# One layernorm's transposes derived from another's in an attention and mixture-of-experts block

## The chip, the cores and the metric

The kernel runs on one core of a Trainium2 chip. The metric is the device time of one execution in microseconds (us), from the device's own clock. A core has five engines that work side by side, each through its own list of instructions in order: TensorE (PE: matmuls and transposes), VectorE (DVE), ScalarE (ACT), GpSimd (POOL) and SyncE (SP). DMA transfers are issued by SP, ACT or POOL and carried out by 16 DMA engines. TensorE writes to PSUM, whose banks of 128 x 512 f32 (the kernel uses eight) must be read out ("evicted") by VectorE or ScalarE before they can be used again.

## What is computed

Everything is f32. x has 2 x 2048 tokens of width 256.

```python
xn = layernorm(x)                                  # first layernorm
# attention: 16 heads of 16, Chebyshev features of order 6, prefix sums instead of a softmax
qkv = xn @ W_in.T ; ... ; attn = (num / den) @ W_out.T
# feed-forward on xn
xf = layernorm(xn) * ln_w + ln_b                   # second layernorm
e = argmax(xf @ router_w) ; s = sigmoid(max(xf @ router_w))
routed = silu((s*xf) @ gate[e]) * ((s*xf) @ up[e]) @ down[e]      # one of 8 experts per token
shared = silu(xf @ sh_gate) * (xf @ sh_up) @ sh_down
out = x + attn + xn + routed + shared
```

With m and v the mean and variance of a token's row, r0 = 1/sqrt(v + 1e-5) is the scale of the first layernorm. The second layernorm, applied to the first's result, is z = (x - m) * r1 with a scale r1 of its own that follows from v alone: r1 = 1/sqrt(v(1 + 1e-5) + 1e-10). So xn and z are the same row (x - m) with two scales, and xn = z * (r0 / r1).

## The kernel before

The 4096 tokens are cut into 8 chunks of 512 (`CH`), each of 4 tiles of 128. Layouts: a tile has tokens on the partitions; matmuls want the features there, so each chunk's z and xn are transposed on TensorE into xfT and xnT (two halves k of 128 features by 512 tokens).

*The front* (L453 to L579), in three groups of chunks, [0], [1, 2, 3] and [4, 5, 6, 7]. `stat` (L455) takes mean and variance on VectorE; `roots` (L464) gets r0 and r1 (`rs`) from a square root on ScalarE and a Newton step on VectorE, and `nm` from them (L486, L487). `front(c)` (L491) makes xn on ScalarE (L499, four activations per chunk) and z on VectorE (L507, into `zall`), transposes both on TensorE (L519: for each of the two, two halves of four 128 x 128 transposes, each half into one PSUM bank), and evicts: xfT on ScalarE with ln_w and ln_b (L523), xnT on ScalarE or VectorE (L527, L529). z goes to DRAM for later gathers (L530), xfT and xnT of chunks 1 to 7 too (L569, L571). The router multiplies xfT for each pair of chunks (L542), transposes the result (L550) and adds the logits on VectorE (L558, L559). X, which collects the output, is set on ScalarE (L564).

*Constants* on GpSimd (L287 to L342): identity, ones, then heads, weigh, shift, spread, upper for the attention and the routing, all at the very start.

*Routing* (`route`, L582) ranks tokens by expert and builds tables of 36 tiles of 128 slots: 28 full tiles with one expert each (`NFULL`) and 8 tiles whose two halves have different experts.

*Attention* (`attend`, L825): per chunk, QKV matmuls (L848), Chebyshev features, prefix scans on VectorE (L915) and small matmuls (L878 to L986).

*Experts* (`expert`, L1012): SP loads the weights of a tile in three pieces of 512 KB per expert (L1030, L1036), out of a pool `w_p` of 8 pieces that grows by 10 when the attention is done; GpSimd gathers z rows (L1041) and scatters the result (L1087); TensorE transposes (L1049), multiplies (L1059, L1080) and transposes (L1072). A tile of two experts loads six pieces and its matmuls have 64 output rows, in pairs. *Shared expert* (`shared`, L785): L794 and L811 per chunk, held back for the last two chunks (`hold`). Last, SP reads the scattered rows, VectorE adds them and SP stores the output (L1107 to L1121).

*Order.* All this is entered as operations with a cost, a priority and the data and buffers that they need; `Plan.order` (L157) lays them out greedily in time and so fixes each engine's list of instructions before anything runs. A lower `prio` comes first; `alt` names a second engine that may take an operation. Once fixed, an engine that waits for one instruction waits with all behind it. Six PSUM banks (`bank_p`) are shared by nearly everything; a bank is free when every operation that uses it is done.

Of the kernel before, what the change touches and what calls it, by code (L numbers as in the profile page):

```python
# [11 lines left out]
F32 = mybir.dt.float32  # L12
I32 = mybir.dt.int32
AF = mybir.ActivationFunctionType
ALU = mybir.AluOpType
# [5 lines left out]
P = 128  # L21
NB, S, D = 2, 2048, 256
# [3 lines left out]
CH = 512  # L26
# [229 lines left out]
def kernel(  # L256
# [25 lines left out]
    y_dram = dram.tile([NTOK, D], F32, name="y_dram")  # L282
    xn_dram = [dram.tile([P, KD, CH], F32, name=f"xn_dram_{c}") for c in range(NC)]
# [9 lines left out]

    heads = const.tile([P, 56], F32, name="heads")
    nc.gpsimd.affine_select(
        out=heads, in_=ones[:, :56], pattern=[[-DH, 56]], compare_op=ALU.is_ge,
        fill=0.0, base=24 * DH, channel_multiplier=1,
    )
    nc.gpsimd.affine_select(
        out=heads, in_=heads, pattern=[[DH, 56]], compare_op=ALU.is_ge,  # L300
        fill=0.0, base=DH - 1 - 24 * DH, channel_multiplier=-1,
    )

    sqb = const.tile([P, 2], F32, name="sqb")
    nc.gpsimd.memset(sqb[:, 0:1], sq4[1])
    nc.gpsimd.memset(sqb[:, 1:2], sq5[1])

    HB = NH // KD  # L310
    weigh = const.tile([P, QD], F32, name="weigh")
    nc.gpsimd.memset(weigh, 0.0)
    for lo, n, base, wt in [(0, NH, QD * i, wts[i + 1]) for i in range(4)] + [
            (g * HB, HB, QD * g + NH, wts[5]) for g in range(KD)]:
        nc.gpsimd.affine_select(
            out=weigh[:, lo : lo + n], in_=weigh[:, lo : lo + n], pattern=[[-1, n]],
            compare_op=ALU.not_equal, fill=wt, base=-base, channel_multiplier=1,
        )

    shift = const.tile([P, 1], F32, name="shift")  # L320
    nc.gpsimd.memset(shift, 0.0)
    nc.gpsimd.memset(shift[QD : QD + NH, :], -DH * off[2])
    nc.gpsimd.memset(shift[3 * QD : 3 * QD + NH, :], -DH * off[4])

    spread = const.tile([P, KD * P], F32, name="spread")
    nc.gpsimd.memset(spread, 1.0)
    for i in range(NT):
        rows = spread[ts(i, QD), :]
        nc.gpsimd.affine_select(
            out=rows, in_=rows, pattern=[[1, KD * P]], compare_op=ALU.is_ge,  # L330
            fill=0.0, base=0, channel_multiplier=-DH,
        )
        nc.gpsimd.affine_select(
            out=rows, in_=rows, pattern=[[-1, KD * P]], compare_op=ALU.is_ge,
            fill=0.0, base=DH - 1, channel_multiplier=DH,
        )

    upper = const.tile([P, P], F32, name="upper")
    nc.gpsimd.affine_select(
        out=upper, in_=ones[:, :P], pattern=[[1, P]], compare_op=ALU.is_gt,  # L340
        fill=0.0, base=0, channel_multiplier=-1,
    )  # L342
# [16 lines left out]
    nm = const.tile([P, 2, NTT], F32, name="nm")  # L359
# [19 lines left out]
    def cut(n):  # L379
        nonlocal at  # L380
        at += n
        return wide[:, at - n : at]

    xn_p = Pool([cut(NT * D) for _ in range(2)])
# [25 lines left out]
    plan.begin["POOL"] = 7.5  # L410
# [42 lines left out]
    xfTs, xnTs, spilled, fronts = {}, {}, [], []  # L453

    def stat(c):  # L455
        for t in range(NT):
            i = c * NT + t

            def f(c=c, t=t, i=i):
                V.bn_stats(stats[:, i, :], X[c][:, t, :])  # L460
                V.bn_aggr(mv[:, i, :], stats[:, i, :])
            op("DVE", 0.58, f, r=[("X", c, t)], w=[("mv", i)], prio=FRONT + 0.1 * c)

    def roots(cs):  # L464
        a, b = cs[0] * NT, (cs[-1] + 1) * NT
        n = slice(a, b)
        keys = [("mv", i) for i in range(a, b)]
        p = FRONT + 0.1 * cs[0] + 0.01

        def f():  # L470
            V.tensor_scalar(ve[:, 0, n], mv[:, n, 1], EPS, None, ALU.add)
            V.tensor_scalar(ve[:, 1, n], mv[:, n, 1], 1.0 + EPS, EPS * EPS, ALU.mult, ALU.add)
        op("DVE", 0.35, f, r=keys, w=[("ve", a)], prio=p)
        op("ACT", 0.21, lambda: A.activation(rs[:, :, n], ve[:, :, n], AF.Sqrt),
           r=[("ve", a)], w=[("rs", a)], prio=p, table="sqrt")

        def h():
            r_, u_, v_ = rs[:, :, n], nu[:, :, n], ve[:, :, n]
            V.reciprocal(r_, r_)

            V.tensor_tensor(u_, r_, r_, ALU.mult)
            V.tensor_tensor(u_, u_, v_, ALU.mult)
            V.tensor_scalar(u_, u_, -0.5, 1.5, ALU.mult, ALU.add)
            V.tensor_tensor(r_, r_, u_, ALU.mult)

            V.scalar_tensor_tensor(nm[:, 0, n], mv[:, n, 0], -1.0, rs[:, 0, n], ALU.mult, ALU.mult)  # L486
            V.tensor_scalar(nm[:, 1, n], rs[:, 0, n], 1.0, None, ALU.add)  # L487
        op("DVE", 1.2, h, r=[("ve", a), ("rs", a)] + keys, w=[("nm", a // NT + k) for k in range(len(cs))],
           prio=p)

    def front(c):  # L491
        xn4 = Buf(xn_p, f"xn_{c}")
        v4 = lambda b: b.t.rearrange("p (t d) -> p t d", t=NT)
        p = FRONT + 0.1 * c + 0.02
        for t in range(NT):
            i = c * NT + t

            def f(t=t, i=i):
                A.activation(v4(xn4)[:, t, :], X[c][:, t, :], AF.Identity,  # L499
                             bias=nm[:, 0, i : i + 1], scale=rs[:, 0, i : i + 1])  # L500
            op("ACT", 0.59, f, r=[("X", c, t), ("nm", c)], w=[(xn4, t)], prio=p,
               alloc=[xn4] if t == 0 else [])
        for t in range(NT):
            i = c * NT + t

            def f(t=t, i=i):
                V.tensor_scalar(zall[:, i, :], X[c][:, t, :], mv[:, i, 0:1], rs[:, 1, i : i + 1],  # L507
                                ALU.subtract, ALU.mult)
            op("DVE", 0.4, f, r=[("X", c, t), ("nm", c)], w=[("z", i)], prio=p)
        xnT, xfT = Buf(xnT_p, f"xnT_{c}"), Buf(xfT_p, f"xfT_{c}")  # L510
        v2 = lambda b: b.t.rearrange("p (k t) -> p k t", k=KD)
        for nx in (1, 0):
            for k in range(KD):
                bk = Buf(bank_p, f"tr_{c}_{nx}_{k}")

                def f(bk=bk, k=k, nx=nx):
                    for t in range(NT):
                        src = zall[:, c * NT + t, ts(k, P)] if nx else v4(xn4)[:, t, ts(k, P)]
                        T_.transpose(bk.t[:, ts(t, P)], src, ident)  # L519
                op("PE", 4 * MT, f, r=[("z", c * NT + t) if nx else (xn4, t) for t in range(NT)],  # L520
                   w=[bk], alloc=[bk], prio=p)
                if nx:
                    op("ACT", 0.65, lambda bk=bk, k=k: A.activation(  # L523
                        v2(xfT)[:, k, :], bk.t, AF.Identity, bias=lnb[:, k : k + 1], scale=lnw[:, k : k + 1]),
                       r=[bk, "ln"], w=[(xfT, k)], alloc=[xfT] if k == 0 else [], prio=p)
                else:
                    op("ACT", 0.58, lambda bk=bk, k=k: A.copy(v2(xnT)[:, k, :], bk.t),  # L527
                       r=[bk], w=[(xnT, k)], alloc=[xnT] if k == 0 else [], prio=p,
                       alt=[("DVE", 0.68, lambda bk=bk, k=k: V.tensor_copy(v2(xnT)[:, k, :], bk.t))])  # L529
# [31 lines left out]
        for t in range(NT):  # L561
            i = c * NT + t
            kw = dict(bias=nm[:, 0, i : i + 1], scale=nm[:, 1, i : i + 1])
            op("ACT", 0.59, lambda t=t, kw=kw: A.activation(X[c][:, t, :], X[c][:, t, :], AF.Identity, **kw),  # L564
               r=[("nm", c)], w=[("X", c, t)], prio=ROUTE + 1.0)
# [8 lines left out]
    for cs in ([0], [1, 2, 3], [4, 5, 6, 7]):  # L574
        for c in cs:
            stat(c)
        roots(cs)
        for c in cs:
            front(c)  # L579


    def route():  # L582
# [64 lines left out]
        op("PE", 0.9, f, r=["m"], w=[rank, total], alloc=[rank, total], prio=R)  # L647
# [137 lines left out]
    def shared(c, gate):  # L785
# [19 lines left out]
        for tp in range(NT // 2):  # L805
            po = Buf(bank_p, f"po_{c}_{tp}")

            def mm(po=po, tp=tp):
                for i in range(2):
                    for f in range(KF):  # L810
                        T_.matmul(po.t[:, ts(i, D)], hT[f].t[:, ts(tp * 2 + i, P)], sd[:, f, :],  # L811
                                  start=(f == 0), stop=(f == KF - 1))
            op("PE", 8 * M256, mm, r=hT + ["sd"], w=[po], alloc=[po], prio=SHA + c - 0.2)
            accumulate(c, tp, po)
# [10 lines left out]
    def attend(c, gate):  # L825
# [9 lines left out]
        for g in range(KD):  # L835
# [7 lines left out]
            for i in range(3):  # L843
# [6 lines left out]
                o = op("PE", 2 * MM, mm, r=[(xnT, 0), (xnT, 1), "w_in"], w=[pm],  # L850
# [161 lines left out]
    def expert(j):  # L1012
        e = 0.1 * j
# [79 lines left out]
    for j in range(NJ):  # L1093
        expert(j)
# [3 lines left out]
    gate, hold = [], {NC - 2: ups[-6], NC - 1: ups[-3]}  # L1098
# [4 lines left out]
    for c in range(NC):  # L1103
# [15 lines left out]
        n = 2 if c == NC - 1 else NT  # L1119
        for t in range(0, NT, n):  # L1120
# [43 lines left out]
```

## Time and profile before

| what | value |
|---|---|
| runs | 587.37, 589.61 and 2120.74 us; median 589.61 |
| profiled execution | 588.28 us, span from first to last instruction 586.6 us |
| granted TensorE clock | 0.999 |
| TensorE's first instruction / last matmul group begins | 8.97 / 575.38 us |
| instructions | 7613 |

Times in the profile are microseconds from the start of the span unless they are marked ns. In lists of engines, each entry is busy time, share of the span and number of instructions. In the view by slices the span is cut into 40 equal parts, and a digit is the busy share in tenths. In the view of waits a line is "who waited <- for whom: us in total, times, longest". In a timeline a line begins with start and duration; `x8` are eight instructions in a row, and an f32 matmul is recorded as two. `out<-in` are buffers; `L519` is the line of the kernel. PEld is the load of a matmul's stationary operand, beside PE. SPq and ACTq are DMA issues.

### The profile page before, as it was taken

The numbers are of one execution on the slowest core, as the hardware profiler recorded it, in microseconds if no ns is written. First come the engines' busy times: TensorE is split into PE (matmuls) and PEld (weight loads), VectorE is DVE, ScalarE is ACT, GpSimd is POOL, SyncE is SP. The second block draws the span as 40 slices with busy tenths as digits, with TensorE's granted clock in tenths as the row PEclk, the third lists the DMA queues.
The fourth block names the chain that finished last, engine by engine and source line by source line (L and its number), as shares of the span: only waits on it lengthen the run. The fifth ranks groups of instructions, "written<-read, shape, count | busy, mean of one in ns | idle before, by whom it ended". The sixth has DMA issues, their size and how long they took to land.

```text
span 586.6 us, 7613 instructions
## 1 busy us (share of the span) xinstructions
PE 570.6 (97%) x2492; PEld 318.8 (54%) x2492; DVE 486.7 (83%) x785; ACT 252.2 (43%) x494; POOL 96.1 (16%) x106
## 2 busy tenths in 40 slices
PE   3999999999999999999999999999999999999997
PEld 2467566746455545656554554564646544644565
DVE  6889889899999989999999999998999898222254
ACT  5799981135533732542364272355236222112100
POOL 4000000302112033003112302311230313010100
PEclk9999999999999999999999999999999999999999
DMA  8788704517374274418525455572652677995096
GB/s 271 237 307 302 284 1 144 195 56 226 98 234 159 93 230 161 148 53 284 186 102 196 161 165 161 189 241 92 196 176 76 186 256 217 359 377 191 0 356 217
DMA packets 73048, 111.15 MB, mean 189 GB/s; under 512 B 5293, under 2 KB 44463, under 8 KB 73008
## 3 DMA queue, kind: packets, MB, share of 16 engines
q1 hardware_dynamic: 68704, 101.72, 52.2%
q0 software_dynamic: 3456, 8.92, 4.6%
q8 instruction: 20, 0.33, 0.2%
q14 instruction: 20, 0.16, 0.1%
q10 hardware_dynamic: 848, 0.01, 0.1%
HBM read 90.71 MB, written 20.45 MB: 190 GB/s over the span
## 4 chain that ended last, share of the span: by engine, by line
PE 62%; DMA 1%; issue 1%; DVE 0%; POOL 0%; POOLq 0%; DVEq 0%
PE bank L1059 16%; PE bank L794 10%; PE bank L1080 9%; PE bank L848 9%; PE bank L811 6%; PE bank L986 4%; PE bank L1072 2%; PE psk L878 2%; PE psq L878 1%; PE bank L1049 1%; DMA wide<-z_dram,take_i 1%; PE psk L891 1%; PE psk L972 1%; PE bank L959 0%; DMA y_dram<-wide,give_i 0%
## 5 line engine op out<-in xcount | busy, mean ns | idle before, releaser
L1059 PE MATMUL bank<-big,wide 128*128 128x512 f32 (+1 forms) x308 | 121.9, 595 | 0.0
L1087 POOL DMA_INDIRECT y_dram<-wide,give_i x34 | 44.1, 1296 | 333.2 <-ACT carry L921 121.7
L848 PE MATMUL bank<-xnT,w_in 128*128 128x512 f32 x192 | 86.5, 594 | 0.0
L915 DVE TENSOR_TENSOR_SCAN tv<-ones,carry,tv 128x512 f32<-128x512 f32 x60 | 76.6, 1277 | 1.1
L1059 PEld LDWEIGHTS bank<-big,wide 128*128 128x128 f32 (+1 forms) x308 | 47.1, 175 | 55.2 <-issue 52.7
L1080 PE MATMUL bank<-big,wide 128*128 128x256 f32 (+1 forms) x312 | 65.1, 385 | 0.0
L794 PE MATMUL bank<-xfT,sg 128*128 128x512 f32 x128 | 60.8, 597 | 0.0
L794 PE MATMUL bank<-xfT,su 128*128 128x512 f32 x128 | 60.7, 596 | 0.0
L1041 POOL DMA_INDIRECT wide<-z_dram,take_i x34 | 41.0, 1206 | 112.6 <-DVE wide L772 102.5
L1080 PEld LDWEIGHTS bank<-big,wide 128*128 128x128 f32 (+1 forms) x312 | 47.5, 175 | 20.7 <-issue 11.5
L811 PE MATMUL bank<-sd,hT 128*128 128x256 f32 x256 | 57.9, 381 | 0.0
L848 PEld LDWEIGHTS bank<-xnT,w_in 128*128 128x128 f32 x192 | 35.7, 190 | 38.2 <-issue 36.1
L811 PEld LDWEIGHTS bank<-sd,hT 128*128 128x128 f32 x256 | 47.8, 190 | 10.7 <-issue 4.5
L1065 ACT ACTIVATE wide<-bank,slot_s 128x512 f32<-128x512 f32 x35 | 24.1, 688 | 65.9 <-PE bank L1059 65.9
L800 ACT ACTIVATE hT<-bank 128x512 f32<-128x512 f32 x32 | 19.1, 597 | 65.2 <-PE bank L794 63.3
L935 DVE TENSOR_TENSOR o<-o,tv 128x512 f32<-128x512 f32 x64 | 44.2, 690 | 1.9
L1067 DVE SCALAR_TENSOR_TENSOR wide<-bank,slot_s,wide 128x512 f32<-128x512 f32 x35 | 25.9, 739 | 17.9 <-PE bank L1059 17.6
L819 DVE TENSOR_TENSOR X<-X,bank 128x512 f32<-128x512 f32 x32 | 21.8, 680 | 22.1 <-PE bank L811 18.4
L870 DVE SCALAR_TENSOR_TENSOR T<-T 128x1024 f32<-128x1024 f32 x32 | 38.1, 1215 | 0.2 <-ACT T L863 0.2
L794 PEld LDWEIGHTS bank<-xfT,sg 128*128 128x128 f32 x128 | 23.0, 190 | 25.3 <-issue 24.5
L794 PEld LDWEIGHTS bank<-xfT,su 128*128 128x128 f32 x128 | 23.1, 190 | 24.3 <-issue 23.5
L1052 ACT ACTIVATE wide<-bank,lnb,lnw 128x128 f32<-128x128 f32 x72 | 29.1, 458 | 10.3 <-PE bank L1049 10.3
(197 smaller groups left out, 813.8 us busy)
## 6 DMA issues: line engine op xcount, KB each, us to landing
big<-in_up_w SPq DMA_DIRECT2D x39, 512.0 KB
big<-in_down_w SPq DMA_DIRECT2D x39, 512.0 KB
big<-in_gate_w SPq DMA_DIRECT2D x38, 512.0 KB
z_dram<-big SPq DMA_DIRECT2D x8, 512.0 KB
X<-in_x SPq DMA_DIRECT2D x7, 512.0 KB
xf_dram<-xfT SPq DMA_DIRECT2D x7, 512.0 KB
xn_dram<-xnT SPq DMA_DIRECT2D x7, 512.0 KB
xfT<-xf_dram SPq DMA_DIRECT2D x7, 512.0 KB
```

Of the source, the lines that this page charges most:

```text
L794: T_.matmul(b.t, wt[:, k, ts(f, P)], vx(k), start=(k == 0), stop=(k == KD - 1))
L811: T_.matmul(po.t[:, ts(i, D)], hT[f].t[:, ts(tp * 2 + i, P)], sd[:, f, :], start=(f == 0), stop=(f == KF - 1))
L848: T_.matmul(pm.t, w_in[:, k, ds(i * D + g * P, P)], xnT.t[:, ts(k, CH)], start=(k == 0), stop=(k == KD - 1))
L870: op("DVE", 1.27, lambda i=i, j=j, q=part: V.scalar_tensor_tensor(q[i](), q[j](), off[i], q[1](), ALU.subtract, ALU.mult), r=[(T, j)] + X2 ...
L915: o_ = op("DVE", 1.25, lambda b=b, i=i, g=g: V.tensor_tensor_scan(b.t, ones[:, 0:1].to_broadcast([P, CH]), b.t, 0.0 if opening else old[:, ...
L935: op("DVE", 0.66, lambda o=o, b=b: V.tensor_tensor(o(), o(), b.t, ALU.add), r=[b, ok], w=[ok], prio=p)
L1041: op("POOL", 1.28, lambda: G.indirect_dma_start(out=zt.t, out_offset=None, in_=z_dram, in_offset=bass.IndirectOffsetOnAxis(ap=take_i[:, j ...
L1052: op("ACT", 0.46, lambda k=k: A.activation(xT.t[:, ts(k, P)], pz.t[:, ts(k, P)], AF.Identity, bias=lnb[:, k : k + 1], scale=lnw[:, k : k + ...
L1059: T_.matmul(b.t[n, :], xT.t[:, ds(k * P + n.start, n.stop - n.start)], wt.t[:, ts(k, FF)], start=(k == 0), stop=(k == KD - 1), skip_group_ ...
L1067: op("DVE", 0.75, lambda: V.scalar_tensor_tensor(sl.t, pu.t, sc(), sl.t, ALU.mult, ALU.mult), r=[pu, zt, sl], w=[sl], prio=EXQ)
L1080: T_.matmul(py.t[n, :D], hmT.t[:, ds(i * P + n.start, n.stop - n.start)], wd.t[:, ts(i, D)], start=(i == 0), stop=(i == KF - 1), skip_grou ...
L1087: y_ins.append(G.indirect_dma_start(out=y_dram, out_offset=bass.IndirectOffsetOnAxis(ap=give_i[:, j : j + 1], axis=0), in_=yt.t, in_offset ...
```

## The change

Four things are changed.

1. xn is no longer made and transposed. `roots` also computes ratio = r0/r1 (from r1 times its argument times r0), ScalarE writes it to DRAM token by token (`ratio_dram`), and reads it back for each chunk as a row of 512 broadcast to 128 partitions (`rows`). xnT is then VectorE's product of the transposed z in PSUM and that row (new L497). z may be made on ScalarE too for chunks 1 to 7, and the xfT eviction may go to VectorE. In chunk 0 the second half of xfT is on VectorE.
2. The constants after `rw` are made later on GpSimd, once `nm` of chunk 0 is there; statistics get an earlier priority; `roots` is cut in two.
3. The eight tiles of two experts no longer come last but are spread among the full ones, and the held chunks of the shared expert wait for other tiles.
4. The last pair of the shared expert's down products is cut into two, each with its own add, and the last two tiles are stored one by one.

In the changed kernel L487 are the transposes, L490 and L492 the xfT evictions, L497 the xnT evictions, L456 and L463 the ratio's write and read, L470 and L474 z, L511 the router's matmuls, L814 and L831 the shared expert, L876 QKV, L906 the head sums, L1077, L1087, L1100 and L1108 the experts' TensorE work.

```diff
+    ratio_dram = dram.tile([NTOK], F32, name="ratio_dram")
...
-    xn_p = Pool([cut(NT * D) for _ in range(2)])
+    ratio_p = Pool([cut(CH) for _ in range(4)])
...
-    plan.begin["POOL"] = 7.5
+    plan.begin["POOL"] = 2.0
...
-            op("DVE", 0.58, f, r=[("X", c, t)], w=[("mv", i)], prio=FRONT + 0.1 * c)
+            op("DVE", 0.58, f, r=[("X", c, t)], w=[("mv", i)], prio=FRONT + 0.1 * c - 0.3)
...
+            V.scalar_tensor_tensor(nm[:, 2, n], mv[:, n, 0], -1.0, rs[:, 1, n], ALU.mult, ALU.mult)
+            V.tensor_tensor(ratio[:, n], rs[:, 1, n], ve[:, 1, n], ALU.mult)
+            V.tensor_tensor(ratio[:, n], ratio[:, n], rs[:, 0, n], ALU.mult)
...
+        op("ACT", 0.45, lambda: A.dma_start(
+            out=ratio_dram[a * P : b * P].rearrange("(t p) -> p t", p=P), in_=ratio[:, n]),
+           r=[("ratio", a)], w=[("ratio_dram", c) for c in cs], nbytes=64 * KiB, prio=p)
...
-                A.activation(v4(xn4)[:, t, :], X[c][:, t, :], AF.Identity,
-                             bias=nm[:, 0, i : i + 1], scale=rs[:, 0, i : i + 1])
...
+        rows = Buf(ratio_p, f"ratio_{c}")
+        op("ACT", 0.4, lambda: A.dma_start(
+            out=rows.t, in_=ratio_dram[c * CH : (c + 1) * CH].unsqueeze(0).to_broadcast([P, CH])),
+           r=[("ratio_dram", c)], w=[rows], alloc=[rows], nbytes=256 * KiB, prio=p)
...
+            if c:
+                op("ACT", 0.59, f_, r=[("X", c, t), ("r", c), ("nm", c)], w=[("z", i)], prio=p, alt=[("DVE", 0.36, f)])
+            else:
+                op("DVE", 0.36, f, r=[("X", c, t), ("r", c)], w=[("z", i)], prio=p)
...
+        for k in range(KD):
+            bk = Buf(bank_p, f"tr_{c}_{k}")
+            def f(bk=bk, k=k):
+                for t in range(NT):
+                    T_.transpose(bk.t[:, ts(t, P)], zall[:, c * NT + t, ts(k, P)], ident)
...
+            op(*on[k if c == 0 else 0], r=[bk, "ln"], w=[(xfT, k)],
+               prio=p if c else -2.0, alt=on[1:] if c else [])
+            op("DVE", 0.69, lambda bk=bk, k=k: V.tensor_tensor(v2(xnT)[:, k, :], bk.t, rows.t, ALU.mult),
+               r=[bk, rows], w=[(xnT, k)], prio=p)
...
+    def constants():
+        ins = nc.gpsimd.affine_select(
+            out=heads, in_=ones[:, :56], pattern=[[-DH, 56]], compare_op=ALU.is_ge,
+            fill=0.0, base=24 * DH, channel_multiplier=1,
+        ).ins
+        tc.add_manual_dep(ins, begun[0].name, mybir.DependencyInfo(
+            mybir.DependencyClass.Sync, mybir.DependencyReason.DATA))
...
+    op("POOL", 6.5, constants, r=[("nm", 0)], w=["constants"], prio=FRONT)
...
+            if (c, tp) == (NC - 1, NT // 2 - 1):
+                for i in range(2):
+                    op("PE", 4 * M256, lambda i=i, mm=mm: mm([i]), r=hT + ["sd"], w=[(po, i)],
+                       alloc=[] if i else [po], prio=SHA + c - 0.2)
+                    op("DVE", 0.42, lambda i=i, po=po, xs=X[c][:, 2 * tp + i, :]: V.tensor_tensor(
+                        xs, xs, po.t[:, ts(i, D)], ALU.add), r=[(po, i)], a=[("X", c, 2 * tp + i)], prio=SHQ)
+                continue
...
-    for j in range(NJ):
-        expert(j)
-    gate, hold = [], {NC - 2: ups[-6], NC - 1: ups[-3]}
+    n2 = NJ - NFULL
+    tiles = sorted(range(NJ), key=lambda j: j if j < NFULL else (j - NFULL + 0.5) * NFULL / n2 - 0.25)
+    for n, j in enumerate(tiles):
+        expert(n, j)
+    gate, hold = [], {NC - 2: ups[-9], NC - 1: ups[-2]}
...
-        n = 2 if c == NC - 1 else NT
-        for t in range(0, NT, n):
+        for t, n in ((0, 2), (2, 1), (3, 1)) if c == NC - 1 else ((0, NT),):
```

## Prediction, made before the changed kernel was run

> **What bounds the kernel now.** I read four views: busy time per engine, the 40 slices, TensorE's waits, and TensorE's timeline for starts.
>
> ```profile
> PE 570.6 (97%) x2492; PEld 318.8 (54%) x2492; DVE 486.7 (83%) x785; ACT 252.2 (43%) x494; POOL 96.1 (16%) x106
> ...
> PE   3999999999999999999999999999999999999997
> ...
> DVE  6889889899999989999999999998999898222254
> ```
>
> TensorE works without a break from the first slice to the last. A busy PE can hide short stalls, because the ends of matmuls are modelled, so I also took distances between starts: a 128x512 record starts every 0.43 us nearly everywhere, which is its own time. The waits say the same:
>
> ```profile
> PE bank L519 <- POOL wide L614: 9.0, 1, 9.0
> PE bank L1049 <- DMA wide<-z_dram,take_i: 2.2, 2, 1.4
> PE bank L1072 <- DVE wide L1067: 0.6, 1, 0.6
> ```
>
> After its first instruction at 8.97 us TensorE stands for 2.8 us in all. So the span is a head (until the first real matmul), the sum of TensorE's instructions, its few stalls, and a tail after its last matmul. VectorE (DVE) is full to nine tenths from 40 to 490 us but idles at the end: it matters only where TensorE's fixed order meets a late result.
>
> **The change, part by part**, against the profiled execution: 588.28 us, span 586.6, so 1.7 lie around it. It sits between the two ordinary runs (587.37 and 589.61; the median, 589.61, is the upper one because of an odd run of 2120).
>
> *1. Transposes.* 64 of the 128 front transposes (L519, those that read xn) go; counted in both kernels' instructions, nothing else on TensorE changes in number.
>
> ```profile
> 8.97 2.20 PE L519 MATMUL bank<-ident,big 128*128 128x128 f32 x8 [8.97 <-POOL wide L614]
> 10.96 1.75 PE L519 MATMUL bank<-ident,wide 128*128 128x128 f32 x8
> 12.54 1.88 PE L794 MATMUL bank<-xfT,sg 128*128 128x512 f32 x4
> 14.26 10.46 PE L848 MATMUL bank<-xnT,w_in 128*128 128x512 f32 x24
> ...
> 51.08 1.04 PE L519 MATMUL bank<-ident,wide 128*128 128x128 f32 x8
> 51.95 1.04 PE L519 MATMUL bank<-ident,big 128*128 128x128 f32 x8
> ```
>
> The first number is the start. Eight take 51.95 - 51.08 = 0.87 us, 0.11 each. Of the 64, 56 lie in the gapless part: 56 x 0.11 = **-6.2**. The other eight (10.96 to 12.54) belong to the head.
>
> *2. Head.* The root chain is slowed by GpSimd's constants: the same multiply takes 0.379 us in the head and 0.183 later.
>
> ```profile
> L481 DVE TENSOR_TENSOR nu<-rs x3: 183/191/379, 6.8 to 44.3; 128x8 f32<-128x8 f32 x1, 128x24 f32<-128x24 f32 x1, 128x32 f32<-128x32 f32 x1
> ```
>
> The late constants free it. rs leaves ScalarE at 6.54 as before (the sqrt table, 4.84 to 6.12, sets that); reciprocal and four steps at the later spacing (0.24, then 0.21 each) let z start at 7.67, not 8.41. Transposes start at about 8.2 and end at 10.4. But then VectorE's order puts two statistics pairs of chunk 1 ahead of its half of xfT, and chunk 1 lands at about 10.55 (L460 waited for it until 10.57; the third pair starts at 11.66). So that half ends at 11.66 + 0.69 = 12.35 and its matmul starts at 12.5, as before; only the matmul of the other half (two records, 0.86) gets done in the gap: -0.9. Against this: row 10.96 shows transposes at 0.20 each, row 12.54 matmuls at full speed, 3.6 us after TensorE's first work. [...] The new head has holes of about 0.8 and 0.4 us in it. [...] The holes are short: I take 0.6. Head: **-0.3** (-0.9 to +0.8).
>
> *3. Half tiles between the others.* A half tile's matmuls use 64 columns in pairs, and going in and out of that form costs time:
>
> ```profile
> 526.24 3.58 PE bank L1059 x16
> 529.83 1.91 PE bank L794 x4
> ...
> 545.56 1.72 PE bank L1059 x4
> ```
>
> 16 half records take 3.58 instead of 16 x 0.215 = 3.44, and the L794 group after them 1.91 instead of 1.72: about 0.34 per stretch. In TensorE's order there are 12 such stretches before and 16 after: 4 x 0.34 = **+1.4**. The stall of 0.8 at 519 us (a gather behind six weight pieces per half tile) should go: **-0.8**. Against that, a half tile takes 6 of the 8 weight pieces that exist during attention, so stalls of that kind can come earlier: -2.5 (the two at 192 and 216 us go) to +4 (half a microsecond on each of eight); I take 0.
>
> *4. The ratio's way through DRAM.* ScalarE loses 32 xn activations (0.59 each) and 4 evictions, gains 8 of z, and issues 11 DMAs at 0.45 us (L426): 5 us, hidden, as it is 43% busy. VectorE evicts all 16 xnT halves (12 before) and 5 of xfT, loses 8 of z at 0.33, and has 9 small steps more: about +5 us in a stage where it isn't full. But two waits are new: ScalarE's read of the rows stands in its queue until the write has landed, and VectorE's xnT eviction stands until the read has. The write is of 4-byte elements: 512, 1536 and 2048 of them, that is 32, 96 and 128 per DMA engine. Rows for the cost:
>
> ```profile
> q1 hardware_dynamic: 68704, 101.72, 52.2%
> ...
> q10 hardware_dynamic: 848, 0.01, 0.1%
> ```
>
> ScalarE's queue (q10) has mostly 4-byte reads: 0.1% x 16 x 586.6 / 848 = 11 ns a packet; SP's (q1) 71 ns. ScalarE's router load was issued at 4.35, 2.2 us after the end of an earlier small one: I take 2.2 us as latency. So the third write lands 2.2 + 128 x 11 ns = 3.6 us after issue. [...] SP's queue is busy then (DMA slices 8 of 10). If each 4-byte packet waits for one of SP's: 128 x 82 ns + 2.2 = 12.7 us; for the groups of 1536 and 512, 10.1 and 4.8 instead of 3.3 and 2.6.
>
> Group 0: issued at about 10.3, rows needed at 25.5 by the first L876; ScalarE must be free for silu by 18.5. Covered either way. Group 1 to 3: ScalarE issues at about 31.7 (after the v eviction of the tenth QKV matmul). TensorE next needs ScalarE behind its read for the bank of row 45, at about 42.2: landed at 35.0 nothing, at 41.8 plus three issues and three activations 2.7 us. Group 4 to 7: here the banks run out. In the new order TensorE's transposes of chunks 4, 5 and 6 fill all six banks, and each bank is kept until xfT and xnT are out of it; the next TensorE instruction (the router's, L511) needs the first of them. I laid VectorE's order end to end with the rows' durations: ratio ready at 47.0; then 13 z (0.33), hT, one xfT, logits, one 1.22 step, and the first xnT ends at 57.7. TensorE comes to the logits' bank at 54.4 (free at 55.7) and to L511 at 56.1 (free at 57.9): 1.3 + 1.8 = 3.1 us idle where before there was none. That is without any late transfer: the write is issued at 49.8, lands at 53.4, the read at 57.0. Landed at 62.4 instead, L511 waits until 67: 11 us. I take 3.1 plus 0.9 for some of the alternation, **+4.0** (0 to +14), nearer to the q10 row because that is the same queue and the same size of element.
>
> *5. Tail.*
>
> ```profile
> 582.49 0.69 DVE L819 TENSOR_TENSOR X<-X,bank 128x512 f32<-128x512 f32 x1 [1.63 <-PE bank L811]
> 583.21 0.37 SPq L1121 DMA_DIRECT2D out<-X  x1
> ```
>
> The last add shrinks from 0.69 to 0.42 and the last store from 256 to 128 KB (at the 359 GB/s of the busy slices 0.36 us less, partly taken by one more issue of 0.37): **-0.5**. Constants on GpSimd: the same work, 2 to 8 us becomes 9 to 16; the first reader is L511 or L906 beyond 40 us, and GpSimd's next job is a gather at 110 us: 0.
>
> Sum: -6.2 - 0.3 + 1.4 - 0.8 + 4.0 - 0.5 = -2.4; 588.3 - 2.4 = 585.9, say **586**.
>
> **Rivals.**
> *A, likeliest:* most of the 7 us of transposes comes back as a bank stall in the front. 586, own range 582 to 590.
> *B, no stall:* VectorE is quicker than I laid it and the rows come in time; 588.3 - 6.4 = 582, with stalls in the experts gone too 579. For it: before, the same stage has no TensorE wait at all. Against it: six banks, six transposes.
> *C, slower:* the 2048 small writes alternate with SP's packets; +14 instead of +4, 596. It has one place, L511 behind the third ratio write. From 3.6 us of landing on, each further microsecond adds one to the end; at about 6 us more the gain is gone. [...]
> *D, slower:* half tiles starve of weights. Three MB per half tile at the 280 GB/s of early slices are 11 us, while 8 pieces let little be fetched ahead; 2 us a tile are +16: 602. Against it: attention leaves 50 us per chunk and its DMA share is only half.
>
> **How the numbers follow.** A 0.55, B 0.20, C 0.17, D 0.08. The time is A's, 586. The range takes in B down to 579 and C up to 597. A measurement of this kernel tells about 2% from no change: under 577.8 or over 601.4 against 589.6. Faster than that needs B with every stall gone and no cold clock: 0.05. Slower: most of D, the end of C: 0.08. Within: 0.87.
>
> **What would show it.** Right: TensorE's busy time about 7 us lower; two or three TensorE waits on VectorE between 50 and 60 us at L511 and L487; first long matmuls at 11 to 12.5 us. ScalarE's wait at L463 tells how long the small writes take: under 4 us speaks for A or B, 8 to 13 for C. Waits of TensorE on weights at L1087 or L1108 speak for D. The prediction is wrong if TensorE's idle time after 9 us is under 2 us, or if the new idle time lies elsewhere than at these lines.

## The result and the profile after

The changed kernel takes **616.43 us** (616.32 to 617.95 in four runs) against 589.48 before (four runs, one more than in the table above): ratio 1.0476, 95% interval 1.0442 to 1.0509. It is 27 us slower; the forecast was 586.0 with a range of 579 to 597. Here and below a ratio is formed from the fast runs alone, without odd or slow ones, and so differs a little from the quotient of the medians. The profiled execution took 616.51 us, its span 614.8 against 586.6.

The page of the changed kernel: busy time per engine, then TensorE, the granted clock and the bytes moved by slices (15.4 us each here), and ScalarE's DMA queue.

```profile
PE 575.5 (94%) x2428; PEld 315.7 (51%) x2428; DVE 490.3 (80%) x795; ACT 232.9 (38%) x460; POOL 94.3 (15%) x106
...
PE   4596849999999999999899989999999999999997
...
PEclk9797959999999999999999999999999999999999
...
GB/s 272 184 56 201 131 371 154 138 92 80 206 136 162 264 188 78 223 299 19 170 264 182 111 211 190 123 247 174 71 255 169 134 188 259 269 351 173 18 274 281
...
q10 hardware_dynamic: 6144, 2.12, 1.5%
```

64 matmul records fewer, and yet TensorE is busy 4.9 us longer. The large holes are all in the first six slices, up to about 92 us, and in the same slices the clock falls: TensorE stands, and when it gets work again it runs at half speed for a while (the granted clock is 0.50 from 24 to 30, 54 to 64 and 78 to 91 us). From the seventh slice on the row looks like that of before. TensorE's waits:

```profile
PE bank L487 <- DVE big L470: 8.2, 1, 8.2
PE bank L814 <- ACT hT L820: 6.4, 1, 6.4
PE bank L487 <- ACT big L474: 6.2, 1, 6.2
PE bank L487 <- ACT T L887: 4.1, 1, 4.1
PE bank L1077 <- DMA wide<-z_dram,take_i: 3.5, 3, 1.6
PE bank L511 <- DVE xnT L497: 3.4, 1, 3.4
PE bank L487 <- DVE xnT L497: 1.8, 1, 1.8
```

The first is the start (9.0 before). The rest, with three smaller ones of 0.5 to 0.9, are 27.5 us where before there were 2.8. That closes the account: 24.7 more waiting, 4.9 more busy time, 0.7 earlier start, 0.5 shorter tail (from the last matmul group's start to the end 10.76 against 11.22) make +28.4; the span grew by 28.2.

Two chains lie behind this. One is the wait that was forecast: ScalarE's read of the rows stands behind the write. ScalarE's timeline (ACTq lines are DMA issues):

```profile
9.64 0.38 ACTq L456 DMA_DIRECT2D ratio_dram<-ratio  x1
...
24.91 0.34 ACTq L463 DMA_DIRECT2D wide<-ratio_dram  x1
25.29 1.28 ACT L820 ACT_TABLE_LOAD   x1 [12.41 <-DMA ratio_dram<-ratio]
26.58 1.08 ACT L820 ACTIVATE hT<-bank 128x512 f32<-128x512 f32 x2
...
41.02 0.37 ACTq L456 DMA_DIRECT2D ratio_dram<-ratio  x1
...
52.66 1.64 ACTq L463 DMA_DIRECT2D wide<-ratio_dram  x3
...
66.57 0.38 ACTq L456 DMA_DIRECT2D ratio_dram<-ratio  x1
...
78.46 0.38 ACTq L463 DMA_DIRECT2D wide<-ratio_dram  x1
```

From the issue of the write to the issue of its read 15.3, 11.6 and 11.9 us pass, for 512, 1536 and 2048 elements. Four times the elements don't take longer: this is no price per packet. Behind the first read stands silu (L820), and behind silu TensorE's 6.4 us at L814. The 4.1 and 6.2 us at L487 stand behind ScalarE's second and third read in the same way, and the 1.8 us for xnT behind the rows, for which VectorE waits 8.8 us.

The other chain does not pass through the ratio's reader. VectorE's statistics wait for x itself:

```profile
13.53 0.18 DVE L420 BATCH_NORM_AGGREGATE mv<-stats 128x2 f32<-128x6 f32 x1
23.26 0.43 DVE L419 BATCH_NORM_STATS2 stats<-X 128x6 f32<-128x256 f32 x1 [9.54 <-DMA X<-in_x]
```

In the kernel before, the same record (chunk 2) starts 7.7 us earlier:

```profile
15.56 0.43 DVE L460 BATCH_NORM_STATS2 stats<-X 128x6 f32<-128x256 f32 x1 [1.57 <-DMA X<-in_x]
```

SP issues these loads, on another queue. What became of them shows in the stretches of 2 us, of which the last three columns are the granted clock, the DMA engines' busy share (it can pass 1) and GB/s. Before:

```profile
16.00:18.00 2.00, 2.00 (x6) 0.93 (x5) 1.66 (x7) 0.70 (x2) 0.00 (x0) 1.00 1.10 348
```

After:

```profile
14.00:16.00 2.00, 2.00 (x3) 0.71 (x3) 0.00 (x0) 0.00 (x0) 1.70 (x6) 1.00 1.64 261
16.00:18.00 2.00, 2.00 (x5) 0.86 (x4) 0.00 (x0) 0.00 (x0) 0.19 (x1) 1.00 1.19 30
18.00:20.00 2.00, 2.00 (x6) 0.95 (x5) 0.00 (x0) 0.00 (x0) 0.00 (x0) 1.00 1.14 49
20.00:22.00 2.00, 0.81 (x2) 0.00 (x0) 0.00 (x0) 0.00 (x0) 0.00 (x0) 1.00 1.29 74
22.00:24.00 2.00, 0.00 (x0) 0.00 (x0) 0.61 (x2) 0.00 (x0) 0.00 (x0) 0.82 0.99 81
...
45.00:50.00 5.00, 5.00 (x24) 3.73 (x22) 4.17 (x13) 0.00 (x0) 0.00 (x0) 1.00 0.64 7
```

The DMA engines count as fully busy and move 30 to 81 GB/s instead of 348, for 8 us, after a write of 2 KB. After the second write it is 7 GB/s, at a busy share of 0.64. I call this the slump.

### The profile page after: what moved, and what is told of

It reads as the page before. It is cut to its first block, busy times and chain, and to the rows that moved or that the text cites. A ratio compares the mean times of both kernels' runs of the same rounds, so it can differ in the third digit from the quotient of the medians.

```text
span 614.8 us, 7469 instructions
## 1 busy us (share of the span) xinstructions
PE 575.5 (94%) x2428; PEld 315.7 (51%) x2428; DVE 490.3 (80%) x795; ACT 232.9 (38%) x460; POOL 94.3 (15%) x106
## 4 chain that ended last, share of the span: by engine, by line
PE 70%; DMA 12%; issue 9%; DVE 5%; ACT 1%; POOL 1%; ACTq 1%; DVEq 0%; POOLq 0%
PE bank L1087 17%; PE bank L814 14%; PE bank L1108 9%; PE bank L876 9%; PE bank L831 8%; DMA ratio_dram<-ratio 6%; PE bank L1014 3%; DMA wide<-z_dram,take_i 3%; DMA y_dram<-wide,give_i 2%; PE bank L1100 2%; PE psk L906 2%; PE psq L906 2%; PE bank L1077 1%; DMA wide<-ratio_dram 1%; PE psk L919 1%
## 5 line engine op out<-in xcount | busy, mean ns | idle before, releaser
L1087 PE MATMUL bank<-big,wide 128*128 128x512 f32 (+1 forms) x320 | 121.5, 599 | 0.0
L876 PE MATMUL bank<-xnT,w_in 128*128 128x512 f32 x192 | 87.4, 596 | 0.0
L1087 PEld LDWEIGHTS bank<-big,wide 128*128 128x128 f32 (+1 forms) x320 | 45.0, 171 | 59.5 <-issue 55.8
L814 PE MATMUL bank<-xfT,sg 128*128 128x512 f32 x128 | 66.0, 641 | 6.9 <-ACT hT L820 6.4
L1069 POOL DMA_INDIRECT wide<-z_dram,take_i x33 | 39.0, 1183 | 149.3 <-DVE give_i L793 139.5
L814 PE MATMUL bank<-xfT,su 128*128 128x512 f32 x128 | 61.8, 606 | 0.0
L831 PE MATMUL bank<-sd,hT 128*128 128x256 f32 x256 | 59.9, 391 | 0.0
L1108 PE MATMUL bank<-big,wide 128*128 128x256 f32 (+1 forms) x304 | 59.0, 384 | 0.0
L831 PEld LDWEIGHTS bank<-sd,hT 128*128 128x128 f32 x256 | 49.7, 197 | 11.5 <-issue 3.8
L876 PEld LDWEIGHTS bank<-xnT,w_in 128*128 128x128 f32 x192 | 35.3, 190 | 37.3 <-issue 35.1
L1108 PEld LDWEIGHTS bank<-big,wide 128*128 128x128 f32 (+1 forms) x304 | 42.9, 170 | 19.4 <-issue 8.8
L820 ACT ACTIVATE hT<-bank 128x512 f32<-128x512 f32 x32 | 19.0, 596 | 80.2 <-PE bank L814 80.2
L814 PEld LDWEIGHTS bank<-xfT,sg 128*128 128x128 f32 x128 | 24.4, 202 | 37.7 <-issue 24.7
L814 PEld LDWEIGHTS bank<-xfT,su 128*128 128x128 f32 x128 | 24.3, 197 | 27.3 <-issue 26.4
L884 ACT ACTIVATE T<-bank 128x512 f32<-128x512 f32 x32 | 19.1, 596 | 42.6 <-PE bank L876 42.2
```

Source lines behind the costliest of these rows:

```text
L814: T_.matmul(b.t, wt[:, k, ts(f, P)], vx(k), start=(k == 0), stop=(k == KD - 1))
L876: T_.matmul(pm.t, w_in[:, k, ds(i * D + g * P, P)], xnT.t[:, ts(k, CH)], start=(k == 0), stop=(k == KD - 1))
L1069: op("POOL", 1.28, lambda: G.indirect_dma_start(out=zt.t, out_offset=None, in_=z_dram, in_offset=bass.IndirectOffsetOnAxis(ap=take_i[:, j ...
L1087: T_.matmul(b.t[n, :], xT.t[:, ds(k * P + n.start, n.stop - n.start)], wt.t[:, ts(k, FF)], start=(k == 0), stop=(k == KD - 1), skip_group_ ...
L1108: T_.matmul(py.t[n, :D], hmT.t[:, ds(i * P + n.start, n.stop - n.start)], wd.t[:, ts(i, D)], start=(i == 0), stop=(i == KF - 1), skip_grou ...
```

## The experiments

Theories after the result: the small writes **clog** the DMA engines, and all loads suffer, whoever reads the ratio; or the **wait** of the ratio's reader is the loss (the mechanism forecast, only longer); or it is the **rest** of the change (fewer transposes in another order of the front, tiles). Ratios below are to the kernel before, on the same chip.

**1. No small write.**

```diff
-        op("ACT", 0.45, lambda: A.dma_start(
-            out=ratio_dram[a * P : b * P].rearrange("(t p) -> p t", p=P), in_=ratio[:, n]),
+        op("ACT", 0.45, lambda: None,
...
-            out=rows.t, in_=ratio_dram[c * CH : (c + 1) * CH].unsqueeze(0).to_broadcast([P, CH])),
+            out=rows.t, in_=one_dram.rearrange("t p -> (t p)").unsqueeze(0).to_broadcast([P, CH])),
```

> The changed kernel without the ratio's small writes: the operation keeps its place in the order but issues nothing, and every chunk's row is read from a small DRAM block of ones that was stored at the start (so xnT is z, not xn; the rest is computed as before). Theory S (the 4-byte writes are the cause): TensorE's idle time in the first 100 us falls from about 27 us (with half clock) to 3 to 5, and the time to 580 to 587 us. Rival Q (the new order itself: six banks full of transposes, VectorE's longer list, half tiles between the others): no write is needed for that, so 605 us or more.

590.45 us, ratio 1.002 (0.9998 to 1.0042). With the write gone, 26 of the 27 us go. It is still 3 us above the 580 to 587 that I expected. TensorE's remaining waits: 5.9 at the gathers, 2.6 at a reload of xfT, 1.4 + 0.2 for VectorE. Taken together, the rest of the change is neither the loss nor a gain.

**2. Small writes that nobody reads.** As 1, with the write put back; the rows are still read from a block of ones.

> As the first, but the 4-byte writes are issued where the changed kernel issues them; nobody reads them, so nobody waits for their landing by data. Theory S1 (the cost is the wait of ScalarE and VectorE for the landing): within 3 us of the first, 580 to 590 us. Theory S2 (the writes clog the DMA engines, so that other transfers are late): chunk 2 of x still lands at 20 us or later (23.3 in the changed kernel, before 15.6), and the time is 592 to 610 us.

612.27 us, ratio 1.0366 (1.0319 to 1.0414). The stretches of this kernel:

```profile
16.00:18.00 2.00, 2.00 (x6) 0.87 (x5) 0.62 (x2) 0.24 (x1) 0.80 (x3) 1.00 1.73 37
18.00:20.00 2.00, 2.00 (x6) 0.95 (x5) 1.67 (x7) 0.60 (x1) 0.00 (x0) 1.00 0.88 88
20.00:22.00 2.00, 2.00 (x6) 0.83 (x5) 0.00 (x0) 0.00 (x0) 0.00 (x0) 1.00 1.11 69
```

The slump is there although nobody reads what is written, and so is most of the loss: 612.27 - 590.45 = **22 us are the clog**. The 616.43 - 612.27 = **4 us** left are what the **wait** for the ratio adds on top (by the ratios 20 and 6). That the 4 us are so few does not mean that nobody waited in the changed kernel: there ScalarE stood until 24.91 us for the first write and VectorE until 23.26 for x, and one wait hides in the other.

Which transfers are late differs. The first tile of chunk 2, which I expected at 20 us or later, is in time here (15.45 us); chunk 3 is not, VectorE's statistics wait 5.4 us for it, until 25.13. And the rows of ones are a load too:

```profile
51.29 1.29 DVE L499 TENSOR_TENSOR xnT<-bank,wide 128x512 f32<-128x512 f32 x2 [6.89 <-DMA wide<-one_dram]
```

TensorE waits 6.2 us for that xnT. So the 22 us hold every late transfer, SP's loads of x and ScalarE's rows; experiment 6 has no rows at all.

**3. The elements 512 bytes apart in DRAM**, nobody reading: as many elements, from the same source.

```diff
-    ratio_dram = dram.tile([NTOK], F32, name="ratio_dram")
+    ratio_dram = dram.tile([NTOK, P], F32, name="ratio_dram")
...
-            out=ratio_dram[a * P : b * P].rearrange("(t p) -> p t", p=P), in_=ratio[:, n]),
+            out=ratio_dram[a * P : b * P, 0:1].rearrange("(t p) o -> p t o", p=P), in_=ratio[:, n].unsqueeze(2)),
```

> As the second, but every 4-byte element goes to a DRAM block of its own, 512 bytes from the next (same number of elements, same size; nobody reads them). Theory L (writes into the same short stretch of DRAM wait for each other; this would explain why 512, 1536 and 2048 elements took nearly the same 15.3, 11.7 and 11.8 us): landing under 6 us, chunk 2 on time, the time that of the first. Theory N (each small write has its price wherever it goes): landing and time as in the second.

594.65 us, ratio 1.0066 (1.0042 to 1.009), 373, 348 and 349 GB/s from 16 to 22 us: no slump.

```profile
18.00:20.00 2.00, 2.00 (x6) 0.80 (x6) 1.83 (x6) 0.25 (x1) 0.00 (x0) 1.00 1.10 348
```

So not the number of small packets makes the slump but that their targets are neighbours. The time is 4 us above that of experiment 1, where I expected the same: so much, at most, is left for the number of packets.

**4. 64 bytes apart, and 16 bytes apart.** As 3, with 16 or 4 elements per row of `ratio_dram` in place of 128.

> As e3_apart512 (small writes that nobody reads, rows of ones), with 64 bytes from element to element instead of 512. If what the writes share is a stretch of up to 64 bytes, the DMA engines keep their rate from 14 to 24 us and the time is e3's, 592 to 596 us; if it is a longer stretch (256 or 512 bytes), part of the slump stays and the time lies between e3's 594.7 and e2's 612.3.

> The kernel with small writes that nobody reads, elements 16 bytes apart in DRAM instead of 4. Apart by 64 bytes it took 591.60 us, adjacent 612.27. If writes conflict by the number that share one stretch of 64 bytes (16 adjacent, 4 here, 1 at 64 bytes), the cost lies between: a landing of 5 to 9 us for the largest group and 593 to 600 us. If conflict is all or nothing for writes in one stretch, it is 607 to 615 us, with landings of 11 to 15 us. If only overlapping neighbours of less than 16 bytes conflict, it is 590 to 593 us.

64 bytes apart: 591.60 us, ratio 1.0066 (1.0041 to 1.0091), landings of 6.4 and 3.7 us, 349 to 372 GB/s from 16 to 22 us. 16 bytes apart: 599.35 us (594.69 to 602.92), ratio 1.0177 (1.0104 to 1.025), landings of 4.6 to 7.5 us; no slump after the first write (336 to 359 GB/s), but 170 GB/s from 40 to 45 and 162 from 65 to 70 us. (Experiment 5, without a slump, moved 186 and 286 there, so only the second figure is clearly low.) So the time is graded: 4, 16, 64 bytes apart give 612, 599, 592 us, ratios of 1.0366, 1.0177 and 1.0066. Stretches of 64 bytes, which hold 16, 4 or 1 of the elements, fit; spacings between 16 and 64 bytes were not tried, and 512 bytes apart was no better than 64 (ratio 1.0066 both).

**5. Runs of 16, 48 and 64 bytes.** Each partition's elements are put side by side in DRAM (nobody reads them), so that a piece of the write is 4, 12 or 16 elements long.

```diff
-            out=ratio_dram[a * P : b * P].rearrange("(t p) -> p t", p=P), in_=ratio[:, n]),
+            out=ratio_dram[:, n], in_=ratio[:, n]),
```

> As e2_nowait (nobody reads what is written), but the ratio is written partition by partition: each partition stores its 4, 12 or 16 values in one run of 16, 48 or 64 bytes, 128 bytes from the next partition, so 128 descriptors per group instead of 512, 1536 and 2048, and 4 writes per 512 bytes instead of 128. If the number of small writes per stretch decides: no slump of the DMA rate, 589 to 595 us. If any write below 512 bytes is enough: 600 us or more.

590.78 us, ratio 1.0041 (1.0026 to 1.0056), no slump (354, 348 and 348 GB/s from 16 to 22 us), landings of 5.1 and 1.4 us. The same bytes, in 128 pieces per write, do next to no harm: short pieces as such are not the cause.

**6. The old kernel with the small writes.** ScalarE issues three writes of the first row of `nm` inside an existing operation, so that every engine's list stays as it was but for these three issues.

```diff
+                if t == 0 and c in (0, 1, 4):
+                    n = slice(c * NT, {0: 4, 1: 16, 4: 32}[c])
+                    A.dma_start(out=ratio_dram[n.start * P : n.stop * P].rearrange("(t p) -> p t", p=P),
+                                in_=nm[:, 0, n])
```

> The kernel before, every engine's list unchanged, plus three writes of 512, 1536 and 2048 neighbouring 4-byte elements (the first row of nm) issued by ScalarE ahead of the xn activations of chunks 0, 1 and 4; nobody reads them. Theory L (neighbouring small writes keep the DMA engines full and stop SP's loads) expects a fall of the DMA rate from 348 to under 100 GB/s in the 10 us after each write and a time 12 to 26 us above before, since 22 us were measured between the new kernel without any small write and the one with writes that nobody reads. The rival, that the writes hurt only together with the new order of the front (bank stall, late statistics), expects the same slump or none, and a time within 3 us of before.

604.70 us, ratio 1.025 (1.021 to 1.0289). The stretches of this kernel:

```profile
14.00:16.00 2.00, 2.00 (x5) 0.91 (x4) 0.00 (x0) 1.71 (x2) 0.00 (x0) 1.00 1.17 69
16.00:18.00 2.00, 2.00 (x6) 0.81 (x5) 0.00 (x0) 0.77 (x2) 0.00 (x0) 1.00 1.22 53
...
40.00:45.00 5.00, 5.00 (x34) 3.16 (x34) 3.43 (x12) 4.19 (x8) 0.00 (x0) 1.00 0.59 23
```

Chunk 2 of x, at 15.56 us before, now comes as late as in the changed kernel:

```profile
23.85 0.43 DVE L461 BATCH_NORM_STATS2 stats<-X 128x6 f32<-128x256 f32 x1 [9.87 <-DMA X<-in_x]
```

SP's stores are late as well: VectorE waits 6.8 us for one of xnT before it can fill that buffer again. Three writes of 2, 6 and 8 KB that nobody waits for cost an otherwise untouched kernel 16 us. The clog is a thing of its own. Why the changed front pays 22 for it and this one 16 no run settles; the late rows of experiment 2 are one thing that this kernel does not have.

**7. The ratio written in rows of 512 bytes.** TensorE transposes the ratio (one instruction per group), ScalarE copies it out of PSUM, and the write has 4, 12 or 16 pieces of 512 bytes; everything else is as changed, though the plan's order shifts a little with the new operations, and the rows are read as meant. I call it kernel 7.

```diff
+        op("PE", 0.12, lambda: T_.transpose(bt.t[:m, :P], ratio[:, n], ident), r=[("ratio", a)], w=[bt],
+           alloc=[bt], prio=p)
+        op("ACT", 0.3, lambda: A.copy(rt.t[:m, :], bt.t[:m, :P]), r=[bt], w=[rt], alloc=[rt], prio=p)
...
-            out=ratio_dram[a * P : b * P].rearrange("(t p) -> p t", p=P), in_=ratio[:, n]),
+            out=ratio_dram[a * P : b * P].rearrange("(t p) -> t p", p=P), in_=rt.t[:m, :]),
```

> The changed kernel with one thing mended: TensorE transposes the ratio (one instruction per group), ScalarE copies it out of PSUM, and the DMA writes rows of 128 tokens, 512 bytes each (4, 12 and 16 descriptors instead of 512, 1536 and 2048). All is computed. Theory S: the write lands in 2 to 4 us, ScalarE's wait for it falls from about 29 us in total to under 4, and the time is 579 to 587 us, less than before. Rival Q: 605 us or more.

**587.45 us**, ratio 0.9953 (0.9934 to 0.9972): 29 us less than the changed kernel, and 0.5% less than before, which is small but clear of 1. Its TensorE waits (in the profiled execution, the fastest of nine at 585.14 us):

```profile
PE bank L492 <- DVE big L475: 8.2, 1, 8.2
PE bank L1082 <- DMA wide<-z_dram,take_i: 4.7, 4, 2.0
PE bank L524 <- ACT tv L520: 0.6, 1, 0.6
PE bank L1113 <- ACT wide L1107: 0.5, 1, 0.5
PE bank L516 <- DVE xnT L502: 0.5, 1, 0.5
PE bank L819 <- DMA xfT<-xf_dram: 0.2, 1, 0.2
```

After the start, the whole front costs 1.3 us of waiting (0.6 + 0.5 + 0.2), and TensorE is busy 565.0 us.

**8. The tiles' order, in both fronts.** Kernel 7 with the old order of tiles and the old holds; and the kernel before with only the new order and holds.

```diff
-    tiles = sorted(range(NJ), key=lambda j: j if j < NFULL else (j - NFULL + 0.5) * NFULL / n2 - 0.25)
+    tiles = list(range(NJ))
...
-    gate, hold = [], {NC - 2: ups[-9], NC - 1: ups[-2]}
+    gate, hold = [], {NC - 2: ups[-6], NC - 1: ups[-3]}
```

> The kernel of e4_rows512 with the experts' tiles in the old order (the eight tiles of two experts last, held chunks as before). My step 3 put the new order at +1.4 for four more stretches of 64-column matmuls and -0.8 for a stall at the end; e4's TensorE waited 4.7 us for gathers, against 2.2 before. Theory T (the new tile order costs more than it brings): 1 to 4 us less than e4, that is 583 to 586 us. Rival U (it is neutral or a gain): e4's 587.5 or more.

> The kernel before with nothing but the new tile order and the new holds. Theory T: 1 to 4 us slower than before, with more waits of TensorE for gathers and 16 instead of 12 stretches of 64-column matmuls. Rival U: the same as before or faster.

Kernel 7 with the old order: ratio 1.0113 (1.0068 to 1.0158), the four runs behind it scattered from 590.24 (granted clock 1.000) to 598.32 us (0.996). The kernel before with the new order: 602.85 us, ratio 1.024 (1.0216 to 1.0264), with these waits:

```profile
PE bank L1049 <- DMA wide<-z_dram,take_i: 11.5, 6, 3.6
PE bank L519 <- POOL wide L614: 8.9, 1, 8.9
```

So the same edit gains some 9 us in one front (by the ratios, 1.0113 against 0.9953; the four runs lie 3 to 11 us above kernel 7's median) and loses 14 in the other. I had expected a loss of 1 to 4 us in both, so I was wrong in sign for the first and in size for the second. In the second, TensorE waits for gathers 11.5 us, 9.3 more than before, and is busy 575.5 us, 4.9 more, of which 4.1 are work at a granted clock below 1 (0.97 from 300 to 350 us and 0.93 from 450 to 500; summed over stretches of 1 us; before there is none). What this trace shows is that gathers on GpSimd come late; why they do so in one order and not in the other stays open, and so does where the first front's gain comes from. No weight load shows among these waits.

## Why the prediction was wrong

**The step that failed is step 4, the ratio's way through DRAM**: +4.0 (0 to +14), where the runs show +26 (616.43 against 590.45). It failed in three places.

*The price.* I took 11 ns a packet from ScalarE's queue, "because that is the same queue and the same size of element". The share behind it is printed as 0.1%, so it is anything from 6 to 17 ns; but that is not the error. That row held reads; no row of before held a 4-byte write with neighbours. Landings of 2.6, 3.3 and 3.6 us were forecast, and the reads could go out after 15.3, 11.6 and 11.9. The other price, each 4-byte packet behind one of SP's, gave 4.8, 10.1 and 12.7. It was an estimate of mine, and the 0.9 us for "some of the alternation" in the +4.0 rest on it; no run shows such an alternation. It is near for two of three, but by luck: I had counted every element as one packet, and a price per packet it cannot be, as the first landing shows (15.3 us for 512 elements, 11.9 for 2048). And the same 4-byte pieces 64 or 512 bytes apart (experiments 4 and 3) land in 3.7 to 6.4 us, runs of 16 to 64 bytes (5) in 1.4 to 5.1: their length does not tell the good ones from the bad; spacing does. What happens inside the engines no run here shows.

*The direction.* This is the larger error. Rival C, too, asked only how late the ratio would be, and so ended at 596. I treated SP's packets as what delays the small writes, not the small writes as what delays SP's packets. 22 of the 26 us come without any reader of the ratio, and 16 us in the kernel before, which has no rows. In both the changed kernel and that one chunk 2 of x comes about 8 us late (23.26 and 23.85 against 15.56); statistics, z and transposes follow. In the changed kernel the granted clock falls to 0.50 after each large hole. The 4 us that the reader's wait adds are, by chance, the number that I had for the step.

A slip in rival C: it says that the gain is gone at about 6 us of further delay. By the prediction's own numbers the gain without any delay is 2.4 + 0.9 = 3.3 us, so 3.3 us would do.

*The bank stall.* 3.1 us were forecast at L487 and L511 even with rows in time. With the write gone it was 1.6 (experiment 1), and with the 512-byte rows 1.1 (0.6 + 0.5, experiment 7). My end-to-end layout of VectorE's order was too slow, so B was nearer than A here.

The other steps:

*1, transposes (-6.2), and the stretches of half tiles (+1.4): they fit.* In kernel 7 TensorE's busy time is 570.6 - 565.0 = 5.6 us lower; all 64 transposes at 0.11 less the 1.4 are 5.6. The 1.4 was not measured alone: in the second kernel of experiment 8, which has the four more stretches and all transposes, 4.9 - 4.1 = 0.8 us are left for it. In the changed kernel the same gain lies under 10.5 us of additional busy time (575.5 - 565.0), 8.2 of it from granted clocks below 1, 1.3 from the slow head.

*2, head: the dates right, the clock wrong.* z starts at 7.69 (7.67 forecast) and transposes at 8.24 (8.2). The shared expert's matmuls begin at 10.97, but slowly. TensorE's timeline of the changed kernel:

```profile
10.97 3.80 PE L814 MATMUL bank<-xfT,sg 128*128 128x512 f32 x4 [0.52 <-ACT xfT L490]
14.56 2.83 PE L814 MATMUL bank<-xfT,su 128*128 128x512 f32 x4
17.22 1.88 PE L814 MATMUL bank<-xfT,sg 128*128 128x512 f32 x4
```

And of kernel 7:

```profile
10.40 3.35 PE L819 MATMUL bank<-xfT,sg 128*128 128x512 f32 x4
13.59 1.88 PE L819 MATMUL bank<-xfT,su 128*128 128x512 f32 x4
```

Four records should take 1.72 us from start to start (17.22 to 18.94 do). Kernel 7's first four take 13.59 - 10.40 = 3.19: 1.5 lost. The changed kernel's first eight take 6.25 instead of 3.44: 2.8 lost. I had counted 0.6 for the short holes, a figure that no run shows; the runs show these 1.5 and 2.8. The granted clock stands at 1.00 in these stretches, so only the durations tell. Before, the slow time fell on 16 transposes (2.20 and 1.75 us for eight each, 1.04 later); with eight of them gone it falls on matmuls. In kernel 7 the first four records end at 13.59, against 14.26 before, so its head still gains 0.7 (forecast 0.3).

*3, half tiles: the sum wrong by 3.3.* -0.8 and 0 were forecast for stalls; in kernel 7 the gathers' waits rose from 2.2 to 4.7 us (+2.5), in experiment 1 to 5.9. This is against the kernel before; in kernel 7's own front the old order is slower still (experiment 8). Rival D looked for stalls of the tiles at their weights; none is there (no wait on weights in the changed kernel or in kernel 7). The tiles wait for gathers.

*5, tail (-0.5): right*, 10.76 against 11.22.

Without the clog the sum comes out near the forecast's -2.4: kernel 7's span is 3.2 us shorter, of which busy time gives -5.6, the start -0.8, the tail -0.5 and waits +3.7. Of the 6.9 us gained, 3.7 went back into waits, 2.5 of them at the gathers. But that is in part luck: less waiting in the front than forecast (1.3 instead of 4.0) makes up for more at the gathers (+2.5 instead of -0.8).

Of the signs named in the prediction, ScalarE's wait at L463 was to tell the length of the writes, and the 12.4, 9.4 and 7.7 us of ScalarE's idle time there spoke for C. Of the 27.5 us of TensorE's idle time only 6.1 (3.4 + 1.8 + 0.9) are waits on VectorE at L511 and L487, where it was forecast; the longest wait is at L814. And TensorE's busy time, which was to fall by 7 us, rose by 4.9. What no sign was set for is SP's queue: a wait of VectorE's statistics on x.

## What to carry to other kernels

Before a small tensor goes to DRAM with its elements scattered over partitions, look at where neighbouring elements come from: 4-byte pieces next to each other, written from different partitions, held up the DMA traffic here, not only their reader (30 to 81 GB/s instead of 348 for 8 us, and 22 us of time with nobody reading them). Give each partition its own run (590.78 us here, though nothing read the ratio), or transpose on TensorE first and write whole rows, which turned 616 us into 587. And when pricing a transfer, ask both ways: what delays it, and what it delays; a row of reads (11 ns a packet) didn't price a write (15.3 us for 512 elements).

## What the hardware showed that I had not expected

- 512 neighbouring 4-byte writes (2 KB) take the DMA rate from 348 GB/s to 30 to 81 for some 8 us, with the engines' busy share at 0.99 to 1.29. The busy share said nothing about bytes there; put it beside the GB/s.
- Their landing does not grow with their number (15.3 us for 512, 11.9 for 2048), but depends on how near they lie to each other: 4.6 to 7.5 us 16 bytes apart, 6.4 and 3.7 us 64 bytes apart, 5.1 and 1.4 in runs.
- After a hole of 6.4 us TensorE's granted clock was at 0.50 from 25 to 30 us, and again from 55 to 63 and from 80 to 90 us: these stalls cost their length and then slowed the work behind them. The first four matmul records after that hole took 3.2 us from start to start instead of 1.72. At the very start, the first four to eight matmul records took nearly twice their time (3.19 us for four, 6.25 for eight) while the granted clock read 1.00.
- One order of tiles gained some 9 us in one front and lost 14 in the other; in the second, TensorE's waits for gathers rose from 2.2 to 11.5 us.
